# Two chained graph layers on one core: the short sums and a set of transposes change their place in each element's first slot, and the end of the last elements is rearranged

## The chip, the cores and the metric

The kernel runs on one core of a Trainium2 chip. The metric is device time in microseconds (us). The program is one launch that works through 32 batch elements. The core has a matrix engine (TensorE, PE in the profile, with its weight loads as PEld), a vector engine (VectorE, DVE), a scalar engine (ScalarE, ACT), GpSimd (POOL, not used in the loop) and SyncE (SP), which issues all transfers.

## The reference, cut to what matters

Everything is float32; a batch has 32 elements, each with 512 rows of 512 columns and a 512 x 512 matrix `adj`.

Layer 0 is attention with 8 heads of 64 columns. From x come q, k and v (products with three weights). The logits are q kᵀ/8 plus log(max(adj, 1e-8)); after the softmax the product with v, the product with Wo, and a layer norm of x plus the result give the rows n.

Layer 1 is graph attention on n with the same `adj`. Each row has one number q and one number k (dot products with two vectors). The logit of a pair is q + k, with (1 - adj) times -1e9 added, then a leaky ReLU with slope 0.01 and a softmax over the row. The weights e, times n, times fc, plus n, are the output:

```
logits = q + swapaxes(k)
masked = logits + (1 - adj) * -1e9
masked = where(masked >= 0, masked, 0.01 * masked)
out    = softmax(masked) @ (n @ fc^T + fc_b) + n
```

## The kernel before, in words

The order of each engine's work is written by hand: inside the kernel the program order of the calls is the order of each engine's queue, and only data dependences (semaphores) hold an engine back. SP's queue of transfers is in that order too.

Each element b has four slots (`slot(b, p)`, p = 0 to 3), one per pair of heads. A slot computes the scores of its pair, in four blocks of 128 keys (`score`, L809: TensorE into a two-bank tile of `ps_s`, then ScalarE's exponential into `at`), multiplies them by adj (`factors`, L823, VectorE; half 0 is blocks 0 and 1, half 1 is blocks 2 and 3) and adds them up over the blocks (`sums`, L833). The product of the factors with v (`values`, L843) comes a slot later: slot p runs `values` of pair p - 1, and slot 0 that of the last pair of element b - 1. Each slot also computes the q and k of the next slot (`seven_qk`, L591), with seven products of half matrices in place of eight (Strassen's scheme, as for v, Wo and fc too); the parts are put together by ScalarE and VectorE. The tile f of these products takes the two `ps_s` tiles of the second scores (blocks 2 and 3), once their exponentials have been read.

The division of the softmax is made once for two pairs. `divide` (L864) sums the 128 partitions of `as` with a weight of ones (TensorE, tile ps: "the short sums"), ScalarE copies them into R, and two small transfers bring them into a compact form c. `divided` (L884) checks their range and takes reciprocals on VectorE, and three transfers spread them to R over all partitions. `scale` (L904) multiplies oT by R. `divide(b, 0)` stands in slot 2 of element b, `divided(b, 0)` in its slot 3; `divide(b, 2)` and `divided(b, 2)` stand in slot 0 of element b + 1, and `scale(b, 2)` in slot 1.

The elements overlap. While slots of element b run layer 0, the same slots hold work of elements b - 1 and b - 2:

- slot 0: the transposes of the second half of adj for b (`turn_a((2, 3))`, VectorE, in place in cT), the transposes of the weights of layer 1 of element b - 2 (`eT`, VectorE, in place in eP) and the product of these weights with n (`z`, TensorE, tile pz, evicted by ScalarE into L), then `rest_of_layer1` (VectorE: `yb` = n * gamma + cc in two operations of 128x2048, and the reciprocals of the sums);
- slot 1: the product with Wo of element b - 1 (`seven_wo`), its statistics for the layer norm;
- slot 2 (`layer1_rows`): the norm's rows of element b - 1, the numbers k and q of its layer 1, the product with fc of element b - 2 (`seven_out`, with two stores of 512 KB), the transposes of x of element b + 1;
- slot 3: v of element b + 1 and the softmax of layer 1 of element b - 1 (`softmax`). That ends with 16 transfers of 64 KB, which rearrange the 32 x 32 blocks of the weights from L1 into eP (`spread_blocks`, L142; at L147). VectorE then transposes within each block.

In slot 0 TensorE's order is: scores 0 and 1, `values` of the last pair, the short sums of element b - 1, scores 2 and 3, the products for q and k, z. VectorE's is: scale, first_difference, factors half 0, turn_a, factors half 1, eT, sums, the additions for q and k, divided, residual, invert.

The last element's fourth slot is `last_slot` (L1186). There is no next element, so what is left of elements 30 and 31 is done: the softmax of layer 1 of element 30, the transposes of its weights on TensorE (pt_e), the division of element 31 without transfers (`divide_here`), z of element 30, Wo of element 31 (`seven_wo` with banks from `other_banks`, L800), its norm and layer 1, and the last two outputs with direct products (`out_units`, L455, tile pg).

`other_banks` gives three banks: b and c are the two halves of one tile of `ps_s`, a is the tile of `ps_o`. A tile is the unit for which one engine waits for another.

`combine_right` (L192) prepares the combinations of fc for the seven products; it also overwrites the upper right quarter of fc by (lower right - upper right). `last_slot` restores that quarter with one subtraction before the direct products.

Of the kernel before, what the change touches and what calls it, by code (L numbers as in the profile page):

```python
# [9 lines left out]
FP = mybir.dt.float32  # L10
# [9 lines left out]
P = 128  # L20
# [10 lines left out]
def kernel(  # L31
# [54 lines left out]
    nc = tc.nc  # L86
# [67 lines left out]
    K = {}  # L154
# [323 lines left out]
    def fast(ctx):  # L478
# [76 lines left out]
        def turn_a(kcs):  # L555
            for kc in kcs:
                nc.vector.transpose(cT[:, kc, :], cT[:, kc, :])
# [242 lines left out]
        def other_banks(b):  # L800

            def tiles():
                f = ps_s.tile([P, 2, N], FP, tag="s", name=f"pw_{b}_bc")
                o = ps_o.tile([P, N], FP, tag="po", name=f"pw_{b}_a")
                return [t.rearrange("p (n f) -> p n f", n=KH)
                        for t in (f[:, 1, :], o, f[:, 0, :])]
            return tiles

        def score(b, p, kc):  # L809
# [54 lines left out]
        def divide(b, p):  # L864


            s = S[b]
            ps = ps_m.tile([P, N], FP, tag="m", name=f"ps_{b}_{p}")
            for h in range(4):
                nc.tensor.matmul(  # L870
                    ps[h * BL : (h + 1) * BL, :], ones[:, :BL], s["as", p + h // 2][:, h % 2, :],
                    start=True, stop=True,
                )
            s["R", p] = act.tile([P, 2, N], FP, tag="R", name=f"R_{b}_{p}")
            r = s["R", p][:, 0, :]
            nc.scalar.copy(r, ps)
            m = 4 * N // P
            d0 = dram.tile([4, N], FP, tag="d0", name=f"d0_{b}_{p}")
            nc.sync.dma_start(out=d0, in_=r.rearrange("(h r) n -> h r n", r=BL)[:, 0, :])
            c = small.tile([P, 2, m], FP, tag="c", name=f"c_{b}_{p}")  # L880
            nc.sync.dma_start(out=c[:, 0, :], in_=d0.rearrange("h (a m) -> (h a) m", m=m))
            s["c", p] = c
# [150 lines left out]
        def slot(b, p):  # L1033

            last, nxt = b - 1, b + 1
            if p == 1 and last >= 0:
                load_n(last)
            if p == 1 and nxt < B:  # L1040
                load_x(nxt)
            if p == 3:
                differences(nxt)
            for kc in (0, 1):
                score(b, p, kc)
            if p == 1 and last >= 0:
                wos, wo_adds = seven_wo(last, long_banks(last))
                run(wos[:1])
            run(values(b, p - 1) if p > 0 else values(last, 3) if last >= 0 else first_v[1:2])
            if p == 0 and last >= 0:  # L1050
                scale(last, 0)
                first_difference(last)
                divide(last, 2)
            factors(b, p, 0)
            if p == 1:
                sums(b, p, 0)
                if last >= 0:
                    scale(last, 2)
                    first_sum(last)
            if p == 2 and last >= 0:  # L1060
                norm = normalise_units(S[last], small, last)
                run(norm[:1])
            if p == 0 and b > 0:
                turn_a((2, 3))
            if p == 3:
                load_a(nxt, (0, 1))
                if last >= 0:
                    mask(S[last])
                if b == 0:
                    run(combine_qk()[1:])  # L1070
            for kc in (2, 3):
                score(b, p, kc)
            soft = softmax(last) if p == 3 and last >= 0 else []
            run(soft[:1])
            factors(b, p, 1)
            if p == 3 and last >= 0:
                divided(b, 0)
            if p == 2:
                divide(b, 0)
            if b == 0 and p < 3:  # L1080
                next_qk = qk(0, p + 1)
            elif p < 3:
                next_qk = seven_qk(b, p + 1)
            else:
                next_qk = seven_qk(nxt, 0)
            if p == 0:
                if b >= 2:
                    run(eT(b - 2))
                sums(b, p, 0)
                if b == 0:  # L1090
                    run(combine(K["wv"], K["v_s"])[:1] + combine_qk()[:1])
                run(next_qk)
                units = z(b - 2) if b >= 2 else [lambda: spread(ps_o)] if b == 1 else first_v[2:]
                run(units[:2])
                if last >= 0:
                    divided(last, 2)
                run(units[2:])
                if b == 1:
                    combine_right(K["fc"], K["fc_s"])
                if b == 0:  # L1100
                    run(combine(K["wv"], K["v_s"])[1:])
                if b >= 2:
                    rest_of_layer1(b - 2)
            if p == 1:
                sums(b, 0, 1)
                if last < 0:
                    sums(b, p, 1)
                    run(next_qk)
                    bias()
                else:  # L1110
                    for i in range(3):
                        wos[i + 1]()
                        run(wo_adds[i])
                        if i == 1:
                            sums(b, p, 1)
                        next_qk[i]()
                    next_qk[3]()
                    wos[4]()
                    run(wo_adds[3])
                    run(stats_units(S[last], small, last))  # L1120
            if p == 2:
                if b == 0:
                    combine_right(K["wo"], K["wo_s"])
                    run(next_qk)
                    run(xT(nxt))
                    sums(b, p, 0)
                    offset()
                    divided(b, 0)
                else:
                    layer1_rows(b, next_qk, norm[1:])  # L1130
            if p == 3:
                load_a(nxt, (2, 3))
                vs = seven_v(nxt)
                vs[0]()
                run(soft[1:2])
                next_qk[0]()
                vs[1]()
                next_qk[1]()
                run(soft[2:])
                sums(b, 2, 1)  # L1140
                vs[2]()
                next_qk[2]()
                next_qk[3]()
                vs[3]()
                turn_a((0, 1))
                sums(b, p, 0)
                sums(b, p, 1)

        def layer1_rows(b, next_qk, norm):

            last, nxt = b - 1, b + 1
            muls, adds = [], [[], [], [], []]
            next_qk[0]()
            run(norm[:2])
            next_qk[1]()
            run(norm[2:])
            sums(b, 2, 0)
            if b >= 2:  # L1160
                z_sums(b - 2)
                muls, adds = seven_out(b - 2)
            ks, qs = dots_units(S[last], small, S[b]["R", 0][:, 1, :], last)
            run(ks)
            store_k(S[last], small, dram, last)
            run(next_qk[2:])
            run(muls[:1] + adds[0])
            turns = xT(nxt) if nxt < B else [lambda: sums(b, 2, 1)]
            run(turns[:1] + muls[1:2] + adds[1][:1] + turns[1:])
            load_k(S[last], work(last)[:, 1, :])  # L1170
            run(adds[1][1:])
            load_e(last, 0)
            run(muls[2:3] + adds[2] + muls[3:])
            load_e(last, 1)
            run(adds[3][:1] + qs)
            if nxt == B:
                load_n(b)
                divided(b, 0)
            run(adds[3][1:])

        def run_out(units):
            for mul, add in units:
                mul()
                add()

        def last_slot():  # L1186


            b, last = B - 1, B - 2
# [2 lines left out]
            run(values(b, 2))  # L1192
            factors(b, 3, 0)
            sums(b, 3, 0)
            mask(S[last])
            for kc in (2, 3):
                score(b, 3, kc)
            factors(b, 3, 1)
            load_e(b)
            vs = values(b, 3)  # L1200
            vs[0]()
            run(softmax(last))
            vs[1]()
            here2, here3 = divide_here(b, 2), divide_here(b, 3)
            here2[0]()
            nc.vector.tensor_add(S[b]["as", 3], S[b]["as", 3], S[b]["at", 3, 2])
# [24 lines left out]
            wos[4]()  # L1231
            run(wo_adds[3])
            invert(S[last])
            fc12, fc22 = K["fc"][:, :KH, H:], K["fc"][:, KH:, H:]
            nc.vector.tensor_sub(fc12, fc22, fc12)
            run(stats_units(S[b], small, b))
            zs[1]()
            norm = normalise_units(S[b], small, b)
# [45 lines left out]
        for b in range(B):  # L1284
            for p in range(NPAIR):
                if b == B - 1 and p == 3:
                    flag = last_slot()
                else:
                    slot(b, p)
        return flag  # L1290


# [142 lines left out]
```

## Time and profile before

| | us |
|---|---|
| three runs | 3533.10, 3531.07, 3532.73 |
| median | 3532.73 |
| profiled execution, its own time | 3532.92 |
| its span, first to last instruction | 3531.1 |
| TensorE busy | 3488.3 |
| VectorE busy | 2817.0 |
| ScalarE busy | 1377.2 |
| from one element to the next, in the middle | 108.62 |

The rows of the profile give an engine, a line of the kernel (L870) and an operation with the tile that it writes and those that it reads. In the timeline each row is a group of like instructions in order of time: start, length, then engine, line, operation, operands, shape, and how many. A bracket at its end is the time for which the engine stood idle before it, and what ended that. In the list of waits the first number is the total in us, then how often, then the longest. A float32 product of 128 x 128 by 512 columns shows as two matmul instructions. The last row of the table is the distance of the first z matmuls of neighbouring elements.

### The profile page before, as it was taken

Reading aid. Unit: us, or ns where it says so; the run is one execution under the profiler, and the core shown is the slowest. Engines: PE = TensorE matmul, PEld = TensorE weight load, DVE = VectorE, ACT = ScalarE, POOL = GpSimd, SP = SyncE. Lnnn points to the kernel's source line nnn. Section 1 sums busy time; section 2 is a strip of 40 time slices with the busy share of each in tenths; the row PEclk is TensorE's granted clock in tenths of the full one; section 3 lists DMA queues with packets and bytes.
Section 4 is the critical chain, followed back from the end, with each engine's and each line's share of the span. In section 5 each row is a group of like instructions: output and inputs, shape, how many; then the busy total and the mean of one; then the engine's idle time right before and its main releaser. Section 6 shows DMA issues by size and latency. Waiting matters only on the chain.

```text
span 3531.1 us, 40900 instructions
## 1 busy us (share of the span) xinstructions
PE 3488.3 (99%) x14554; PEld 2196.2 (62%) x14554; DVE 2817.0 (80%) x4925; ACT 1377.2 (39%) x2339; POOL 0.9 (0%) x9
## 2 busy tenths in 40 slices
PE   9999999999999999999999999999999999999998
PEld 3666666665666566666666666566656666666654
DVE  6878888778877788787888877887778878788875
ACT  3343343334433443434334333444344343434432
POOL 0000000000000000000000000000000000000000
PEclk9999999999999999999999999999999999999999
DMA  4334343343333343333434234333334242343420
GB/s 114 53 60 87 64 81 64 55 87 81 65 75 61 69 87 64 76 64 60 87 64 81 63 55 87 82 63 76 62 67 87 62 78 64 59 87 64 81 75 28
DMA packets 880010, 250.82 MB, mean 71 GB/s; under 512 B 806716, under 2 KB 806972, under 8 KB 879800
## 3 DMA queue, kind: packets, MB, share of 16 engines
q1 hardware_dynamic: 879800, 248.15, 36.1%
q8 instruction: 117, 1.92, 0.2%
q14 instruction: 93, 0.76, 0.1%
HBM read 181.93 MB, written 34.65 MB: 61 GB/s over the span
## 4 chain that ended last, share of the span: by engine, by line
PE 75%; DVE 12%; SPq 5%; issue 3%; DMA 2%; ACT 2%; DVEq 0%; ACTq 0%
PE f L604 14%; PE pz L310 13%; PE sc L815 10%; PE po L853 9%; PE pw_a L205 6%; PE pw_o_a L205 4%; SPq L147 4%; DVE at L828 4%; PE pw_c L205 3%; PE pw_o_c L205 3%; PE pv_a L205 3%; PE pw_o_b L205 2%; DVE eP L535 2%; DMA eP<-L 2%; PE pw_b L205 2%
## 5 line engine op out<-in xcount | busy, mean ns | idle before, releaser
L828 DVE SCALAR_TENSOR_TENSOR at<-cT,at 128x1024 f32<-128x1024 f32 x512 | 600.9, 1215 | 278.8 <-ACT at L820 275.2
L820 ACT ACTIVATE at<-sc 128x1024 f32<-128x1024 f32 x512 | 496.7, 1022 | 601.5 <-PE sc L815 599.8
L815 PE MATMUL sc<-qT,kT 64*128 64x512 f32 x2048 | 509.9, 616 | 2.2 <-DVE kT L639 2.2
L853 PE MATMUL po<-at,v 128*64 128x512 f32 x2048 | 468.6, 599 | 0.9 <-DVE at L828 0.9
L310 PE MATMUL pz<-eP,n 128*128 128x512 f32 x960 | 420.0, 595 | 11.8 <-DVE eP L535 11.8
L815 PEld LDWEIGHTS sc<-qT,kT 64*128 64x128 f32 x2048 | 176.5, 186 | 284.3 <-issue 284.3
L853 PEld LDWEIGHTS po<-at,v 128*64 128x64 f32 x2048 | 135.6, 137 | 319.0 <-issue 313.9
L310 PEld LDWEIGHTS pz<-eP,n 128*128 128x128 f32 x960 | 179.9, 190 | 239.1 <-issue 215.2
L841 DVE TENSOR_TENSOR as<-as,at 128x1024 f32<-128x1024 f32 x254 | 310.2, 1222 | 5.4
L604 PE MATMUL f<-xT,wq 128*128 128x256 f32 x992 | 261.0, 386 | 8.3 <-ACT at L820 8.3
L604 PE MATMUL f<-T,qk_s 128*128 128x256 f32 x992 | 246.2, 381 | 0.0
L452 ACT COPY L<-pz 128x512 f32<-128x512 f32 x128 | 74.9, 586 | 418.9 <-PE pz L310 418.9
L604 PEld LDWEIGHTS f<-xT,wq 128*128 128x128 f32 x992 | 183.4, 190 | 82.4 <-ACT at L820 60.0
L604 PEld LDWEIGHTS f<-T,qk_s 128*128 128x128 f32 x992 | 185.7, 190 | 30.2 <-ACT at L820 5.8
L861 ACT COPY oT<-po 128x512 f32<-128x512 f32 x128 | 75.2, 588 | 287.6 <-PE po L853 287.6
L838 DVE TENSOR_TENSOR as<-at,at 128x1024 f32<-128x1024 f32 x128 | 153.8, 1201 | 1.1
L744 DVE TENSOR_TENSOR n<-pw_a,n 128x512 f32<-128x512 f32 x96 | 66.3, 691 | 99.4 <-PE pw_a L205 99.4
L627 ACT ACTIVATE qT<-f,bq 128x256 f32<-128x256 f32 x124 | 58.3, 470 | 220.3 <-PE f L604 220.3
L633 ACT ACTIVATE kT<-f,bk 128x256 f32<-128x256 f32 x124 | 58.5, 472 | 196.4 <-PE f L604 196.4
L604 PE MATMUL f<-xT,qk_s 128*128 128x256 f32 x496 | 127.3, 379 | 0.0
L604 PE MATMUL f<-T,wk 128*128 128x256 f32 x496 | 127.3, 379 | 0.0
L604 PE MATMUL f<-xT,wk 128*128 128x256 f32 x496 | 127.3, 379 | 0.0
(239 smaller groups left out, 5350.5 us busy)
## 6 DMA issues: line engine op xcount, KB each, us to landing
cT<-in_adj_dram SPq DMA_DIRECT2D x512, 64.0 KB
R<-d SPq DMA_DIRECT2D x126, 256.0 KB
x<-in_x_dram SPq DMA_DIRECT2D x124, 256.0 KB
n<-in_x_dram SPq DMA_DIRECT2D x31, 1024.0 KB
L<-in_adj_dram SPq DMA_DIRECT2D x60, 512.0 KB
eP<-L SPq DMA_DIRECT2D x480, 64.0 KB
out_dram<-yb SPq DMA_DIRECT2D x60, 512.0 KB
w<-dk SPq DMA_DIRECT2D x32, 256.0 KB
```

What stands on the lines that cost most here:

```text
L147: nc.sync.dma_start(out=dst[j * BL : (j + 1) * BL, :, :].rearrange("r c (t q f) -> q r (c t) f", q=P // BL, f=BL)[i], in_=src[i * BL : (i ...
L205: nc.tensor.matmul(to[:, n, :], data(i, c)[:, ts(n, P)], weights[i][:, c, :], start=(first and n == 0 and c == 0), stop=(n == KH - 1 and c ...
L310: nc.tensor.matmul(ps, lhs(i), rhs(i), start=(i == 0), stop=(i == 3))
L452: nc.scalar.copy(s["zT"][:, d, :], pz)
L604: nc.tensor.matmul(to, left[i][:, c, ts(p, P)], s["B"][i][:, c, :], start=(first and c == 0), stop=(c == KH - 1), skip_group_check=True,)
L815: nc.tensor.matmul(sc[:, j, :], s["kT", p][rows, ts(kc, P)], s["qT", p][rows, :], start=True, stop=True,)
L820: nc.scalar.activation(at, sc, AF.Exp, scale=SCALE)
L828: nc.vector.scalar_tensor_tensor(at, cT[:, kc, :].unsqueeze(1).to_broadcast([P, 2, N]), ADJ_MIN, at, ALU.max, ALU.mult,)
L838: nc.vector.tensor_add(s["as", p], s["at", p, 0], s["at", p, 1])
L841: nc.vector.tensor_add(s["as", p], s["as", p], s["at", p, kc])
L853: nc.tensor.matmul(s["po", p][j * DK : (j + 1) * DK, :], s["v"][h // 4][:, kc, ts(h % 4, DK)], s["at", p, kc][:, j, :], start=(kc == 0), s ...
L861: nc.scalar.copy(s["oT"][p], s["po", p])
```

## The change

Three things are done.

In slot 0, for every element after the first, `divide` of the element before and `turn_a((2, 3))` move from ahead of the second scores to behind them, and `eT` moves from behind the second factors to ahead of turn_a. VectorE's order becomes: scale, first_difference, factors half 0, eT, turn_a, factors half 1, sums, the additions for q and k. TensorE's becomes: scores 0 and 1, values, scores 2 and 3, the short sums, q and k, z. `divided` moves from behind the second z unit to the end of the slot, behind `rest_of_layer1`.

At the last element, slot 2 leaves out the seven products for the output of element 29 (and the two sums on z that they need) and computes that output with `out_units`, four direct rows with one store of 256 KB each. Three rows run in slot 2, the fourth in `last_slot`. The upper right quarter of fc is restored at the start of that slot 2. The weights' input e of element 30 is loaded in one transfer instead of two. In `last_slot` the mask of element 30 goes behind the second factors, and both halves of the last product with v go ahead of its softmax.

`other_banks` takes three tiles: a and b are the first banks of two `ps_s` tiles, c is the tile of `ps_o`.

```diff
         def other_banks(b):
 
             def tiles():
-                f = ps_s.tile([P, 2, N], FP, tag="s", name=f"pw_{b}_bc")
-                o = ps_o.tile([P, N], FP, tag="po", name=f"pw_{b}_a")
-                return [t.rearrange("p (n f) -> p n f", n=KH)
-                        for t in (f[:, 1, :], o, f[:, 0, :])]
+                f = [ps_s.tile([P, 2, N], FP, tag="s", name=f"pw_{b}_{i}")[:, 0, :] for i in "ab"]
+                o = ps_o.tile([P, N], FP, tag="po", name=f"pw_{b}_c")
+                return [t.rearrange("p (n f) -> p n f", n=KH) for t in (f[1], f[0], o)]
             return tiles
...
             if p == 0 and last >= 0:
                 scale(last, 0)
                 first_difference(last)
-                divide(last, 2)
             factors(b, p, 0)
...
-            if p == 0 and b > 0:
-                turn_a((2, 3))
...
             soft = softmax(last) if p == 3 and last >= 0 else []
             run(soft[:1])
+            if p == 0 and last >= 0:
+                if b >= 2:
+                    run(eT(b - 2))
+                turn_a((2, 3))
+                divide(last, 2)
             factors(b, p, 1)
...
             if p == 0:
-                if b >= 2:
-                    run(eT(b - 2))
                 sums(b, p, 0)
...
-                run(units[:2])
-                if last >= 0:
-                    divided(last, 2)
-                run(units[2:])
+                run(units)
...
                 if b >= 2:
                     rest_of_layer1(b - 2)
+                if last >= 0:
+                    divided(last, 2)
...
-                    layer1_rows(b, next_qk, norm[1:])
+                    return layer1_rows(b, next_qk, norm[1:])
...
             last, nxt = b - 1, b + 1
+            if nxt == B:
+                fc12, fc22 = K["fc"][:, :KH, H:], K["fc"][:, KH:, H:]
+                nc.vector.tensor_sub(fc12, fc22, fc12)
...
-            if b >= 2:
+            if b >= 2 and nxt < B:
                 z_sums(b - 2)
                 muls, adds = seven_out(b - 2)
...
             run(next_qk[2:])
+            if nxt == B:
+                outs = out_units(S[b - 2], out[b - 2], ps_m, b - 2)
+                sums(b, 2, 1)
+                outs[0][0]()
+                load_k(S[last], work(last)[:, 1, :])
+                load_e(last)
+                load_n(b)
+                outs[0][1]()
+                run_out(outs[1:2])
+                run(qs)
+                divided(b, 0)
+                run_out(outs[2:3])
+                return outs[3]
...
-        def last_slot():
+        def last_slot(rest):
...
             sums(b, 3, 0)
-            mask(S[last])
             for kc in (2, 3):
                 score(b, 3, kc)
             factors(b, 3, 1)
             load_e(b)
+            mask(S[last])
             vs = values(b, 3)
             vs[0]()
+            vs[1]()
+            rest[0]()
             run(softmax(last))
-            vs[1]()
+            rest[1]()
...
-            fc12, fc22 = K["fc"][:, :KH, H:], K["fc"][:, KH:, H:]
-            nc.vector.tensor_sub(fc12, fc22, fc12)
             run(stats_units(S[b], small, b))
```

More of the change, by code (lines that the diff above doesn't have):

```diff
@@ L1166, in layer1_rows @@
             run(next_qk[2:])
+            if nxt == B:
[11 more added lines that the diff above has]
+                return outs[3]
             run(muls[:1] + adds[0])
-            turns = xT(nxt) if nxt < B else [lambda: sums(b, 2, 1)]
+            turns = xT(nxt)
             run(turns[:1] + muls[1:2] + adds[1][:1] + turns[1:])
@@ L1174, in layer1_rows @@
             load_e(last, 1)
[L1175 to L1179, printed above, removed]
+            run(adds[3][:1] + qs + adds[3][1:])
         def run_out(units):
@@ L1286, in fast @@
                 if b == B - 1 and p == 3:
-                    flag = last_slot()
+                    flag = last_slot(rest)
                 else:
-                    slot(b, p)
+                    rest = slot(b, p)
         return flag
```

## The prediction

> **What bounds the kernel now.** I read the page first. TensorE is busy in 99% of the span and has most of the chain that ended last; no other engine comes near.
>
> ```profile
> PE 3488.3 (99%) x14554; PEld 2196.2 (62%) x14554; DVE 2817.0 (80%) x4925; ACT 1377.2 (39%) x2339; POOL 0.9 (0%) x9
> ```
>
> So the span moves only with TensorE's own order of work, and 1% of idle time looks like all there is to win. The list of waits, read next, says otherwise. Its columns are total us, times, longest; there are 32 batch elements.
>
> ```profile
> PEld ps L870 <- DVE as L841: 19.8, 31, 0.6
> ...
> PE pz L310 <- DVE eP L535: 11.8, 30, 0.4
> PE f L604 <- ACT at L820: 8.3, 31, 0.3
> ```
>
> Three waits come once per element, and the first is one of the weight load, inside a stretch that counts as busy. All three lie in the first slot (p = 0). The timeline of TensorE there, element at 1062 us (start, length, then the group):
>
> ```profile
> 1067.64 1.84 PE L870 MATMUL ps<-as,ones 128*32 128x512 f32 x8
> 1069.41 1.99 PE L815 MATMUL sc<-qT,kT 64*128 64x512 f32 x8
> 1071.66 1.13 PE L604 MATMUL f<-xT,wq 128*128 128x256 f32 x4 [0.27 <-ACT at L820]
> ...
> 1074.41 1.03 PE L604 MATMUL f<-xT,wq 128*128 128x256 f32 x4
> 1075.28 1.03 PE L604 MATMUL f<-T,wk 128*128 128x256 f32 x4
> 1076.14 1.03 PE L604 MATMUL f<-xT,qk_s 128*128 128x256 f32 x4
> 1077.00 1.03 PE L604 MATMUL f<-xT,wk 128*128 128x256 f32 x4
> 1078.42 14.00 PE L310 MATMUL pz<-eP,n 128*128 128x512 f32 x32 [0.39 <-DVE eP L535]
> ```
>
> The third slot (p = 2) of the same element already has the order that the change gives the first: second scores, short sums, then the next q and k.
>
> ```profile
> 1014.99 1.99 PE L815 MATMUL sc<-qT,kT 64*128 64x512 f32 x8
> 1016.90 1.07 PE L870 MATMUL ps<-as,ones 128*32 128x512 f32 x8
> 1017.90 1.13 PE L604 MATMUL f<-xT,wq 128*128 128x256 f32 x4
> 1018.87 1.89 PE L604 MATMUL f<-T,qk_s 128*128 128x256 f32 x8
> 1020.59 1.03 PE L604 MATMUL f<-xT,wq 128*128 128x256 f32 x4
> ...
> 1024.05 1.89 PE L205 MATMUL pw_o_a<-fc,L 128*128 128x256 f32 x8
> ```
>
> Start to start, the same sums take 1.00 us there against 1.77, and no score waits. VectorE in the first slot:
>
> ```profile
> 1070.16 2.35 DVE L828 SCALAR_TENSOR_TENSOR at<-cT,at 128x1024 f32<-128x1024 f32 x2
> ...
> 1072.43 1.29 DVE L557 STREAM_TRANSPOSE cT<-cT 128x512 f32<-128x512 f32 x2
> ...
> 1073.65 2.31 DVE L828 SCALAR_TENSOR_TENSOR at<-cT,at 128x1024 f32<-128x1024 f32 x2
> ...
> 1075.89 2.48 DVE L535 STREAM_TRANSPOSE eP<-eP 128x512 f32<-128x512 f32 x4
> ...
> 1094.59 2.36 DVE L828 SCALAR_TENSOR_TENSOR at<-cT,at 128x1024 f32<-128x1024 f32 x2 [8.97 <-ACT at L820]
> ```
>
> It is late for the transposes of eP, yet stands idle 8.97 us before the next slot: its order is wrong, not its load. Last, the end of the program, where TensorE is not full:
>
> ```profile
> 3442.50 0.33 PE L303 MATMUL pt_e<-ident,qk_s 128*128 128x128 f32 x1 [2.62 <-ACT qk_s L431]
> ...
> 3458.49 1.99 PE L205 MATMUL pw_bc<-wo,oT 128*128 128x256 f32 x8 [1.44 <-DVE n L744]
> ```
>
> [...]0.64 us of waiting hides in a busy stretch of 1.84 us.[...] here banks b and c lie in one tile (pw_bc), and TensorE waited 1.44 and 1.38 us for VectorE to read it.[...] the clock reads 1.00 in all 110-us stretches between 220 and 3410 us and 0.93 in 3431 to 3480, where after the wait of 2.62 us four instructions of sums took 1.98 us, before it 1.03.[...]
>
> **The change, part by part.** Times are those of the element at 1062 us.
>
> *Short sums behind the second scores (31 elements).* They wait for the head sums of the last pair, which VectorE ends at 1068.36. Moved behind the scores they start at 1067.64 + 1.92 = 1069.56, later than that: 1.77 becomes 1.00, -0.77. In their new place they fill the time in which the first q/k group waited for ScalarE to empty the scores' banks: scores to that group is 2.25 us now, 1.91 + 1.00 there, so -0.34 beyond the sums themselves; the second group takes 1.78 now, 1.72 there, -0.06. Together -1.17 (6.77 us from 1067.64 to 1074.41; 5.60 in slot 2). ScalarE's copy of the sums goes behind two exponentials, as in slot 2, where nothing waits for it. The two small transfers behind it are issued about 1 us later and needed only when the reciprocals are taken.
>
> *eP's transposes ahead of the second factors (30 elements).* They start where the transposes of cT did, at 1072.43, and end 2.48 us later at 1074.9. z's first matmul would be free at 1067.64 + 2.91 + 6.15 = 1076.70 (both spans from slot 2), so it waits no more: 1.42 us from the last q/k group to z become 0.87, -0.55. The condition is that the 16 block transfers have landed: the last issue ends at 1069.49, and in windows of half a us over all 30 elements their traffic ends by 10.0 us after the slot's first score (1072.1) in most and by 11.0 in all; z feels it from 12.1. Behind the waiting transposes stand those of cT, the second factors, one sum and the three additions to q and k. The second transposes of cT and the second factors end 2.5 us later (1078.5), covered by z's 14 us: the next scores want the banks that the additions free at 1090.6, the product with v reads the factors at 1096. Without that cover each us late would cost one.
>
> Sum: -1.72, taken as -1.71, times 30 = -51.3 us.
>
> *Reciprocals behind the residual.* VectorE's work in the slot is the same, so `divided` ends at 1085.7 instead of 1081.06. It took 5.4 us from there until R had landed (traffic gone at 1086.5), so R is there at 1091.1; scaling in slot 1 now begins at 1098.12, then 1096.4. Margin 5.3 us, cost nothing. On SP only the loads of n and x are queued behind R's two issues; n waits for z until 1090.7, and R is issued by 1088.5.
>
> *Element 1* has no z to hide it: four operations of 2.65 us (`combine_right`) go ahead of `divided`, and R took 6.5 us there (123.98 to 130.47) and already held VectorE 0.35 us. New end 125.65, R at 132.1, scaling done at 133.4; the second weight product wants it at 131.1. Loss 2.3, less the 1.17 of the first part: +1.2 us.
>
> *Last elements.* Element 29's output is now four direct rows of 3.48 us (32 instructions of pg took 14.11) instead of seven products of 1.73 (12.96 with waits): three rows, 10.45, in slot 2 (-2.5) and the fourth in the hole of 2.62 us. That is 1.9 us more for TensorE, but what bounds here is the softmax of element 30 on VectorE. It loses z's two sums, has four operations on the output for sixteen, and one mask (1.22) no longer ahead of the factors; it gains the subtraction on fc (0.66) early, which stood before the statistics. But ScalarE now copies oT first (ready at 3435.4): I get logits 0.8 us earlier. The whole e and n are loaded some 7 us sooner on SP, with their readers at 3434 and later; four stores of 256 KB take the place of two of 512. Filling the hole spares the half clock. With three tiles, the second waiting for both tiles of sums to be read (over by 3452 now), the waits of 1.44 and 1.38 go; then VectorE's row of adds and residuals, some 12 us, sets the pace. The statistics start at about 3468.2 instead of 3472.67: -4.5 us, bounds -7 and +2 (the extra product uncovered), and all behind follows.
>
> Sum: -51.3 + 1.2 - 4.5 = -54.6 us, on the profiled execution 3531.1 of span and 3532.92 in all. The median of the runs, 3532.73, is within 0.2 of that: 3478.1.
>
> **Rivals.**
> A, eP lands late. VectorE then waits at the transposes and z starts no earlier. For: SP issues these 16 without a pause and they are in the chain that ended last. Against: 11.0 us at most, 12.1 to be felt. Price 30 x 0.55: 3494.6.
> B, the gain is given back at another wait, such as TensorE for VectorE in the next slot. For: VectorE has no gap in this slot. Against: 8.97 us of idle time before slot 1, of which 1.7 go. Time about 3529.
> C, slower: R lands late. Its place is the scaling ahead of the second weight product in slot 1. It decides from 5.3 us late, and the kernel is slower than before from 5.3 + 54.6/30 = 7.1. That needs R's transfers stuck behind the 1 MB of n and the blocks of x; 8 us late gives 30 x (2.7 - 1.71) - 3.3 = +26: 3559. Against: R is issued first, and with x issued right behind it at element 1 it was 1.1 us slower, not 7.
>
> **How the numbers follow.** Forecast 0.76 (its own range 3471 to 3486: 0.15 us per element and 3 at the end), A 0.13, B 0.06, C 0.05. The range 3468 to 3496 takes in the forecast and A. A measurement of this kernel can tell about 0.2%, 7 us. Faster: 0.76 + 0.13 + a third of B = 0.91; same: the rest of B, 0.04; slower: C, 0.05.
>
> **What would show it.** Right: sums of 1.07 us behind the scores in slot 0, no wait of f for ScalarE nor of pz for eP, a period of 106.9 instead of 108.6 us, VectorE idle some 7.3 us before slot 1, no wait of pw on pw_b or pw_c. Wrong: a wait for eP's transfers at L535 on VectorE (A), of oT for R (C), or a clock below 1.00 in the middle: at 0.983 the whole gain is gone.

## The result and the profile after

The changed kernel takes 3475.75 us (median of four runs, 3474.64 to 3476.18), against 3532.45 for the kernel before (four runs, 3531.07 to 3533.10): a ratio of 0.984, 95% interval 0.9822 to 0.9857. The forecast was 3478.1 in a range of 3468 to 3496. The profiled execution has a span of 3473.5 us, 57.6 less than before.

The page of the changed kernel, its rows of busy time and of the chain that ended last (before, TensorE had 75% of that chain and VectorE 12%):

```profile
PE 3451.6 (99%) x14530; PEld 2193.0 (63%) x14530; DVE 2813.1 (81%) x4911; ACT 1375.9 (40%) x2338; POOL 1.0 (0%) x9
...
PE 97%; DVE 2%; DMA 1%; ACT 0%; issue 0%; SPq 0%; DVEq 0%; ACTq 0%
```

TensorE's busy share reads 99% as before, though 36.7 us of busy time are gone: 24 of them are the short sums (67.1 us for 504 instructions, 91.0 before). The waits of TensorE, longest first (total us, times, longest):

```profile
PE pt_x L551 <- DMA n<-in_x_dram: 3.6, 1, 3.6
PE pw_c L205 <- DVE oT L921: 2.7, 1, 2.7
PE pt_e L303 <- ACT qk_s L431: 2.5, 4, 1.4
PE sc L814 <- DVE kT L639: 2.2, 1, 2.2
PE pt_e L303 <- ACT cT L431: 1.9, 4, 0.8
```

No wait comes once per element any more; f for the exponential and pz for eP are gone from the list, and so is the weight load of the sums for `as`. TensorE in slot 0, in the timeline of an element in the middle (start, length, group):

```profile
1048.22 1.99 PE L814 MATMUL sc<-qT,kT 64*128 64x512 f32 x8
1050.14 3.65 PE L852 MATMUL po<-at,v 128*64 128x512 f32 x16
1053.72 1.99 PE L814 MATMUL sc<-qT,kT 64*128 64x512 f32 x8
1055.64 1.06 PE L869 MATMUL ps<-as,ones 128*32 128x512 f32 x8
1056.64 1.13 PE L604 MATMUL f<-xT,wq 128*128 128x256 f32 x4
1057.61 1.89 PE L604 MATMUL f<-T,qk_s 128*128 128x256 f32 x8
...
1061.92 1.03 PE L604 MATMUL f<-xT,wk 128*128 128x256 f32 x4
1062.79 13.90 PE L310 MATMUL pz<-eP,n 128*128 128x512 f32 x32
1076.61 1.99 PE L814 MATMUL sc<-qT,kT 64*128 64x512 f32 x8
```

From the slot's first score to z are 14.57 us; before, 16.28. VectorE in the same slot:

```profile
1056.25 2.35 DVE L827 SCALAR_TENSOR_TENSOR at<-cT,at 128x1024 f32<-128x1024 f32 x2
1058.52 2.48 DVE L535 STREAM_TRANSPOSE eP<-eP 128x512 f32<-128x512 f32 x4
1060.93 1.26 DVE L557 STREAM_TRANSPOSE cT<-cT 128x512 f32<-128x512 f32 x2
1062.12 2.31 DVE L827 SCALAR_TENSOR_TENSOR at<-cT,at 128x1024 f32<-128x1024 f32 x2
...
1071.49 0.25 DVE L893 RECIPROCAL c<-c 128x16 f32<-128x16 f32 x1
1078.84 2.36 DVE L827 SCALAR_TENSOR_TENSOR at<-cT,at 128x1024 f32<-128x1024 f32 x2 [7.10 <-ACT at L819]
...
1082.38 1.28 DVE L907 TENSOR_TENSOR oT<-oT,R 128x512 f32<-128x512 f32 x2
```

The transposes of eP follow the first factors without a wait here and end 1.8 us before z begins. (In a few of the 30 elements VectorE waits for eP's transfers after all, 1.2 us in sum and 0.6 at most; z starts 14.56 us after the first score there too.) The idle time before slot 1 is down from 8.97 to 7.10 us: that is the room that the gain came from. The scaling by R does not wait.

At the end of the program, the transposes of elements 30 and 31 (TensorE, same view):

```profile
3387.28 0.33 PE L303 MATMUL pt_e<-ident,qk_s 128*128 128x128 f32 x1 [1.36 <-ACT qk_s L431]
...
3389.40 2.92 PE L303 MATMUL pt_e<-ident,qk_s 128*128 128x128 f32 x13 [0.38 <-ACT qk_s L431]
...
3437.34 3.04 PE L303 MATMUL pt_e<-ident,cT 128*128 128x128 f32 x13 [0.38 <-ACT cT L431]
```

The hole ahead of the first is 1.36 us instead of 2.62. The last group took 1.66 us before and takes 3.04 now.

Where the 57.6 us of span came from:

| part | before | after | gain |
|---|---|---|---|
| one element to the next (eight periods, z to z) | 108.616 | 106.789 | 1.83 x 30 = 54.8 |
| element 1, its first score to that of element 2 | 89.04 | 89.06 | 0.0 |
| last z of eP to the end (the gain without the 0.1 in z itself) | 171.73 | 167.98 | 3.6 |
| start to the first score of element 1 | 104.17 | 104.86 | -0.7 |

The last row has nothing of the change in it: with the same start, the other kernels of this study read 103.7 to 104.8 there.

### The profile page after: what moved, and what is told of

The parts are those of the page before. It is cut to its first block, busy times and chain, and to the rows that moved or that the text cites. A ratio compares the mean times of both kernels' runs of the same rounds, so it can differ in the third digit from the quotient of the medians.

```text
span 3473.5 us, 40744 instructions
## 1 busy us (share of the span) xinstructions
PE 3451.6 (99%) x14530; PEld 2193.0 (63%) x14530; DVE 2813.1 (81%) x4911; ACT 1375.9 (40%) x2338; POOL 1.0 (0%) x9
## 4 chain that ended last, share of the span: by engine, by line
PE 97%; DVE 2%; DMA 1%; ACT 0%; issue 0%; SPq 0%; DVEq 0%; ACTq 0%
PE f L604 22%; PE sc L814 14%; PE po L852 13%; PE pz L310 12%; PE pw_a L205 6%; PE pv_a L205 5%; PE pw_o_a L205 4%; PE pw_c L205 3%; PE pv_b L205 3%; PE pv_c L205 3%; PE pw_o_b L205 3%; PE pw_o_c L205 3%; PE ps L869 2%; PE pw_b L205 2%; PE pg L310 1%; PE pk L310 0%
```

## The experiments

The theory: the two moves in slot 0 release the same z from two sides, TensorE's and VectorE's, and only together give 1.83 us; the later place of `divided` is covered by other work; the end is worth 3 to 4 us. Rivals: the parts add up one by one; the transfers of eP or of R set the time.

### The sums alone, the transposes alone

```diff
                 first_difference(last)
-                divide(last, 2)
...
             run(soft[:1])
+            if p == 0 and last >= 0:
+                divide(last, 2)
             factors(b, p, 1)
```

> Of the change only this: the short sums go behind the second scores in slot 0; VectorE's order and everything else stay as before. Theory (the two moves in slot 0 interlock): the wait of the sums' weight load and the 0.27 us of f for ScalarE go, so q and k are done 1.17 us earlier, but VectorE ends the transposes of eP at the same time as before, so z starts no earlier: the wait of pz for eP grows from 0.39 to about 1.6 us, and the time stays within 4 us of before (about 3531). Rival (the parts add up): 1.17 us for each of 31 elements, about 3496.

Measured: 3532.88 us, ratio 0.9999 (0.9991 to 1.0008). TensorE in slot 0 of this kernel:

```profile
1067.10 1.07 PE L870 MATMUL ps<-as,ones 128*32 128x512 f32 x8
1068.09 1.13 PE L604 MATMUL f<-xT,wq 128*128 128x256 f32 x4
...
1075.96 14.00 PE L310 MATMUL pz<-eP,n 128*128 128x512 f32 x32 [1.56 <-DVE eP L535]
```

The sums are as short as in the whole change and f waits for nothing, but z now waits 1.56 us for eP. From the first score (1059.68) it is 16.28 us to z, to the hundredth what it was before. So 1.17 us for each of 30 elements were won and lost again 8 us later: a second wait stood behind the first.

```diff
             if p == 0 and b > 0:
+                if b >= 2:
+                    run(eT(b - 2))
                 turn_a((2, 3))
...
             if p == 0:
-                if b >= 2:
-                    run(eT(b - 2))
                 sums(b, p, 0)
```

> Of the change only this: eP's transposes go ahead of those of cT and of the second factors on VectorE; the short sums stay ahead of the second scores. Theory: only z's wait goes, 0.55 to 0.66 us for each of 30 elements: 3513 to 3516, with the sums still at 1.84 us. Rival (the blocks of eP land late): VectorE waits at the transposes and z starts as before, about 3532.

Measured: 3513.29 us, ratio 0.9946 (0.993 to 0.9961).

```profile
1060.12 1.84 PE L870 MATMUL ps<-as,ones 128*32 128x512 f32 x8
...
1064.14 1.13 PE L604 MATMUL f<-xT,wq 128*128 128x256 f32 x4 [0.27 <-ACT at L820]
...
1070.34 13.90 PE L310 MATMUL pz<-eP,n 128*128 128x512 f32 x32
```

z starts 15.72 us after the first score (1054.62), 0.56 sooner, and takes 0.1 less itself: 0.66 x 30 = 20 us. One part is worth 0, the other 20 us, both 54 (next run, which also has the reciprocals' move; that is worth nothing at these elements, as shown further below). The additive rival, 3496 for the sums, is excluded.

### All of slot 0, and the end alone

The first of these kernels has the whole diff for slot 0 and nothing of the end; the second is its complement.

> All of the change in slot 0 (sums, transposes, reciprocals at the end of the slot), and the end of the last elements as before. Theory: 30 elements at 1.8 us, element 1 at nothing: 3478 to 3480, so that the end is worth 3 to 4 us in the whole change. Rival: the end carries more than 8 us of the change, because it works with the new order: above 3484.

> The end of the last elements as changed (direct rows for element 29, three bank tiles), and slot 0 as before. Theory: 3 to 4 us faster, 3528 to 3530. Rival: the direct rows (1.9 us more of TensorE) and the new half clock at the end eat it, within 1 us of before.

Measured: 3479.38 us, ratio 0.985 (0.9835 to 0.9865), and 3528.72 us, ratio 0.9987 (0.998 to 0.9993). Against the 3533.04 of the kernel before in these runs that is 53.7 and 4.3 us, in sum 58.0, and the whole change is worth 56.7 or 57.3, by either measurement of the kernel before: these two parts, which lie at different places, add up within the spread of the runs.

### When eP's blocks have landed

```diff
                 first_difference(last)
+                if b >= 2:
+                    run(eT(b - 2))
             factors(b, p, 0)
...
             if p == 0 and last >= 0:
-                if b >= 2:
-                    run(eT(b - 2))
                 turn_a((2, 3))
```

> The whole change, with eP's transposes moved up once more, ahead of the first factors of slot 0. This measures when the blocks have landed: VectorE should stand idle at L535 for eP's transfers in each of 30 elements, some 1.7 to 2.5 us, ending about 10 to 10.5 us after the slot's first score. Theory: covered all the same (z needs the transposes done 14.56 us after that score), time within 3 us of the change, 3473 to 3479. Rival (VectorE's order in slot 0 has no such room): each us of idle time costs up to one, 3500 and more.

Measured: 3477.85 us, ratio 0.9843 (0.9828 to 0.9859). VectorE's waits at these transposes come to 49.5 us in 30 elements, at most 2.8; its timeline in one of them:

```profile
1061.38 2.49 DVE L535 STREAM_TRANSPOSE eP<-eP 128x512 f32<-128x512 f32 x4 [1.76 <-DMA eP<-L]
```

The slot's first score was at 1051.52, so the blocks were there after 9.86 us, in the worst element about 10.9. In the change the transposes are called for after 10.3. Standing idle 1.65 us on average cost nothing: from one element to the next it is 106.79 us in both kernels. (The median is 2.1 us above the change's. In the profile it is element 1 that takes longer, by 3.4 us; nothing of the move lies there.) So rival A of the prediction is out, and VectorE's order in this slot has the room that was claimed.

### R late

```diff
                 if b >= 2:
                     rest_of_layer1(b - 2)
+                    for _ in range(9):
+                        nc.vector.tensor_add(S[last]["R", 2][:, 1, :], K["gamma"], K["cc"])
                 if last >= 0:
                     divided(last, 2)
```

The additions write a half of R that the transfers behind the reciprocals overwrite. The second kernel has 12 of them.

> The whole change, with nine needless additions of 128x512 (0.69 us each, 6.2 us) on VectorE ahead of the reciprocals in slot 0, so that R lands 6.2 us later for 30 elements; they end before VectorE's next work. The prediction put the margin at 5.3 us. Theory: VectorE then waits 0.5 to 1.2 us for R at the scaling, but the second weight product wants it only 2 us after that, so TensorE loses nothing: within 4 us of the change, up to 3480. Rival (each us over the margin is a us lost): 0.9 us for each of 30, about 3503.

> As with nine, but twelve additions, 8.3 us: R 8.3 us later, and VectorE about 1.2 us late for the first factors of slot 1. Theory: now TensorE waits for the scaled oT in slot 1, about 0.9 us at the second weight product and up to 1 us behind it: 3500 to 3535. Rival: still covered, within 4 us of the change.

Measured: 3505.73 us, ratio 0.992 (0.9904 to 0.9935), and 3589.76 us, ratio 1.0155 (1.014 to 1.0171). Both theories fell: with nine the rival's figure held (3503), and twelve cost 55 us more than the upper end of its range. VectorE and TensorE with nine:

```profile
1087.94 0.25 DVE L893 RECIPROCAL c<-c 128x16 f32<-128x16 f32 x1
...
1094.99 1.29 DVE L907 TENSOR_TENSOR oT<-oT,R 128x512 f32<-128x512 f32 x2 [2.49 <-DMA R<-d]
```

```profile
1096.76 1.97 PE L205 MATMUL pw_c<-wo_s,oT 128*128 128x256 f32 x8 [0.70 <-ACT pw_b L697]
```

The reciprocals end 29.93 us after the slot's first score, 6.4 later than in the change. But R then takes 6.8 us to land, not 5.4. Its two transfers are issued from 1089.64 to 1090.94 here, directly ahead of those of n and x (at 1091.04 and 1091.68); whether that is why, no run isolates. So VectorE waits 2.5 us where the margin of the prediction gave 1.1; the weight product was wanted at 1095.90 and starts 0.86 late. (The profile names ScalarE here, whose copy into pw_b ended just before. But in the change this product starts while that copy has yet to begin, so it doesn't need it, and at 26 of 32 such waits with nine additions the profile names VectorE's L921, the differences behind the scaling.) 30 us in all, 1.0 per element. With twelve the reciprocals are 8.6 us late:

```profile
1120.20 2.52 PE L205 MATMUL pw_c<-wo_s,oT 128*128 128x256 f32 x8 [2.68 <-DVE oT L921]
1122.51 1.91 PE L604 MATMUL f<-xT,wq 128*128 128x256 f32 x4
```

To the wait of 2.68 comes here a loss of clock: four matmuls take 1.91 us instead of 1.03. Over the whole of this run the mean clock is 0.992, in the change 0.999. My range had counted 1.9 us per element; it is 3.8, of which the waits are 2.9. The kernel becomes slower than before between 6.4 and 8.6 us of lateness, which takes in the 7.1 of the prediction (rival C); its price for 8 us late, 3559, left out this loss of clock and R's longer landing (6.6 us here: the reciprocals end at 1111.85, the scaling starts at 1118.43).

### The reciprocals' place, and element 1

At element 1 the four operations on fc stand ahead of the reciprocals, and TensorE waited there 2.71 us. This kernel mends that alone:

```diff
                 if b == 1:
+                    divided(last, 2)
                     combine_right(K["fc"], K["fc_s"])
...
-                if last >= 0:
+                if b >= 2:
                     divided(last, 2)
```

> The whole change, but at element 1 alone the reciprocals stand ahead of the four operations on fc again. Theory: R lands there before the second weight product wants it, TensorE's wait of 2.71 us goes; but in the changed kernel this wait had been followed by no half clock at element 1's third slot, which in the kernel before cost 1.6 us, and that may come back: 0.5 to 3 us faster than the change, 3472 to 3475. Rival (the time at element 1 is set elsewhere): no difference, 3475 to 3476.

Another puts `divided` back to its old place at all elements:

> The whole change, but with the reciprocals in their old place (behind z's second unit, ahead of the residual) for all elements. Theory: moving them cost nothing but at element 1, so the time is that of the run that mends element 1 alone, within 2 us. Rival: behind the residual they cost something at every element (or they gained something there): more than 5 us away from that run.

Measured: 3473.01 us, ratio 0.9829 (0.9815 to 0.9842), and 3475.49 us (3472.47 to 3475.86), ratio 0.9835 (0.9821 to 0.9848). The medians lie 2.5 us apart, the spans of the profiled executions 0.6 (3471.2 and 3471.8), the intervals overlap. The medians miss the 2 us of my theory by half a us and stay within the 5 of the rival; the traces decide: from one element to the next both take 106.79 us, as the change does, so the place of the reciprocals costs nothing at every element. The mended element 1 in TensorE's timeline:

```profile
131.08 1.97 PE L205 MATMUL pw_c<-wo_s,oT 128*128 128x256 f32 x8
...
164.66 3.55 PE L814 MATMUL sc<-qT,kT 64*128 64x512 f32 x8 [2.18 <-DVE kT L639]
```

The wait of 2.71 us is gone, and half of it comes back: behind the wait of 2.18 us at the third slot, which all kernels have, the scores take 3.55 us here, 1.99 in the change and 3.10 before (the section on the clock has the clock of these two). From first score to first score element 1 takes 87.84 us, 1.2 less.

### One tile for two banks

`other_banks` as before, all else as changed.

> The whole change, but with the banks b and c of the last Wo product in one tile again. Theory: TensorE's two waits for VectorE to read that tile (1.44 and 1.38 us) come back, but VectorE's row of adds and residuals behind them has some slack, so 1.5 to 2.8 us slower than the change: 3477 to 3479. Rival: VectorE sets the pace there in any case: no difference to the change (3475 to 3476).

Measured: 3479.05 us, ratio 0.9847 (0.9834 to 0.986), 3.3 us above the change. Both waits are back:

```profile
3401.22 1.99 PE L205 MATMUL pw_bc<-wo,oT 128*128 128x256 f32 x8 [1.44 <-DVE n L744]
...
3406.32 1.99 PE L205 MATMUL pw_bc<-wo,oT 128*128 128x256 f32 x8 [1.38 <-DVE n L744]
```

From the last z of eP to the end this kernel takes 171.14 us, the change 168.0. So the 2.8 us of waits cost their whole length, a little more than the range of my theory, and are most of what the end gains: the statistics start 2.3 us later, and then VectorE waits another 1.1 for TensorE's z, which is late too. (The spans of the two profiled executions, 3475.3 and 3473.5, differ by less, because element 1 happened to start 1.2 us sooner here.) The intervals of the ratios overlap, the times themselves don't: 3477.1 is the lowest here, 3476.18 the highest of the change.

### The clock at the end

Four needless matmuls fill the gaps in which TensorE waits for the weights of element 31:

```diff
+                    nc.tensor.matmul(warm, ident, K["wq"][:, 0, :], start=True, stop=True)
                     for c in range(4):
                         nc.tensor.transpose(pt[:, ts(c, P)], s["e"][:, c, ts(0, P)], ident)
+                        if c < 3:
+                            nc.tensor.matmul(warm[:, :200], ident, K["wq"][:, 0, :200], start=True, stop=True)
```

> The whole change, with four needless matmuls put into the four gaps in which TensorE waits for the last element's weights to be exponentiated (0.75 and three times 0.38 us). Theory: the half clock after these gaps (13 transposes in 3.04 instead of 1.66 us, the first z row 3.90 instead of 3.69) comes from the idle time; filled, it stays at full clock: 1 to 2 us faster, 3473.5 to 3475. Rival: the transposes wait for ScalarE's copies, or the clock falls all the same: no difference or slower, 3475 to 3477.

> Element 1 mended and the gaps at the end filled, both on top of the change. Theory: the two gains add up, 2 to 5 us faster than the change, 3471 to 3474. Rival: [...]together they bring no more than one of them.

Measured: 3475.02 us, ratio 0.9835 (0.9821 to 0.9848), on the border of the theory and its rival, and with element 1 mended too 3471.97 us, ratio 0.9826 (0.9813 to 0.9839). The transposes of the first:

```profile
3438.67 0.33 PE L973 MATMUL pt_warm<-ident,cT 128*128 128x128 f32 x1
3438.84 1.50 PE L303 MATMUL pt_e<-ident,cT 128*128 128x128 f32 x12
3440.17 3.69 PE L310 MATMUL pz<-eT,n 128*128 128x512 f32 x8
```

From the first transpose to z are 3.62 us instead of 4.94. In the times the gain of 1.3 us is no more than their spread (in this profile the second weight product of element 1 took 3.64 us, 1.97 in the change's). Both mends together are the fastest kernel of the study, 3.8 us below the change; the intervals of the ratios still overlap.

In the change these 13 transposes take 3.04 us. The view of stretches gives busy time of TensorE, its weight load, VectorE, ScalarE and GpSimd, then the clock, and two columns on transfers. The stretch of the transposes in the change, then in the kernel with eP's transposes first, whose end is the same:

```profile
3437.34:3440.76 3.42, 3.42 (x14) 3.16 (x15) 1.23 (x2) 2.11 (x4) 0.00 (x0) 0.50 0.41 153
```

```profile
3439.86:3443.27 3.41, 2.92 (x17) 2.14 (x18) 1.22 (x3) 2.82 (x7) 0.00 (x0) 1.00 0.40 154
```

The gaps ahead are nearly the same (1.9 and 2.0 us in the lists of waits), and the clock read 0.50 in one trace and 1.00 in the other. In the kernel before, with a longer first gap (1.25 us and three times 0.38), it read 1.00 too, and the same transposes took 1.66 us. With the gaps filled it reads 1.00 from 3435.3 to 3441.3; that the filling kept it up can't be told from these kernels. The same holds at element 1's third slot. Behind the same wait of 2.19 us, in the kernel before and in the change:

```profile
166.56:169.97 3.41, 3.41 (x10) 0.92 (x8) 3.34 (x8) 2.05 (x2) 0.00 (x0) 0.50 0.15 44
```

```profile
167.37:170.78 3.41, 2.61 (x12) 1.12 (x14) 3.41 (x7) 1.44 (x2) 0.00 (x0) 1.00 0.02 5
```

What decides whether the clock falls, no run isolates.

## Why the prediction was right

**Sums behind the scores, -1.17.** The sums now take 1.06 where 1.00 was counted from start to start, f waits no more, and the second group follows in 0.97: as worked out. What the working left unsaid is that this part alone is worth nothing, because z would have waited for eP in its stead. The two amounts were priced one after the other and summed; the sum held only because both moves are in the change.

**Transposes ahead of the second factors, -0.55.** As worked out: z follows the last q/k group after 0.87 us. Mis-sized was z itself: its first matmul had taken 697 ns instead of 592, a part of the wait that counts as busy, so the whole of z went from 13.93 to 13.82. 1.71 was predicted for both, 1.83 measured: 3.5 us over 30 elements.

**Landing of eP.** Predicted by 10.0 us in most and 11.0 in all, 12.1 to be felt; measured 9.86 in one and 10.9 in the worst.

**Reciprocals behind the residual, 0.** They end 23.5 us after the slot's first score (1071.74 against 1048.22), the 23.56 of the prediction, and nothing waits for R. The margin of 5.3 us held by luck, from two errors. With nine additions R took 6.8 us to land instead of 5.4, so VectorE's scaling has a margin of only 3.9 us. But the second weight product is wanted 1.6 us after the scaling could first have served it (in the trace with nine additions, 1095.90 against an estimated 1094.27), so TensorE loses time only from about 5.5 us on, by this estimate.

**Element 1, +1.2.** (2.3 less 1.17 is 1.1.) The wait was 2.71 us against 2.3. R landed as predicted, 28.0 us after the element's first score; but the second weight product waits not only for the scaling, as counted, but for the first of the differences behind it (L921; the product starts 0.5 us after the scaling's end). Still the element lost nothing: before, a half clock had followed the wait at its third slot (clock 0.50, scores of 3.10 and products of 4.19 us), and in the changed kernel it did not (1.00, 1.99 and 3.65). That term was not in the sum, and it is luck: nothing in the change aims at it, and with element 1 mended the scores take 3.55 us again.

**Last elements, -4.5.** Measured -3.6. The statistics start 108.36 us after the last z of eP began, 113.30 before: 4.9 sooner, against 4.5 predicted. The step that failed is "filling the hole spares the half clock". The hole shrank to 1.36 us and three gaps of 0.38, and behind them the clock still read 0.50, for 3.42 us (from 3389.55) where it had been 6.83 (from 3443.35 in the kernel before); and at the very end, where the clock had been full, it fell too, which took back 1.6 us (1.4 in the transposes, 0.2 in z). The latter is chance rather than the change: in the kernel with eP's transposes first, whose end is the same, the clock stayed at 1.00 there and the stretch from the last z took 166.4 us instead of 168.0.

Sum: -51.3 + 1.2 - 4.5 = -54.6 predicted; -54.8 + 0.0 - 3.6 = -58.4 measured by parts, with 0.7 of the start on the other side. Rivals A and B did not come; C needs the reciprocals to be about 7 us later than the change has them. That measurement and forecast lie as close as 2.4 us owes something to chance: the terms that were off (z itself, element 1, the end, the start) are of that size and go both ways.

## What to carry to other kernels

When two engines meet at one instruction, ask of each move what the other engine will hold back instead: here one move alone was worth 0, the other 20 us, and both 54. A busy share of 99% can hide such room; compare a stretch with another stretch of the same kernel that does the same work in a better order, and price the difference from start to start. Before putting a step later, look not only at how long its transfers take now but at which transfers will then be issued beside them (with n and x issued right behind, R took 6.8 us here instead of 5.4).

## What the runs showed that I had not expected

The clock of TensorE read 0.50 for 3.4 us behind idle time shorter than that, and not each time: behind a wait of 2.2 us at one and the same place of element 1 eight scores took 1.99 us in the change, 2.49 with both mends, 3.10 in the kernel before and 3.55 with element 1 mended. Gaps of 0.75 and three times 0.38 us, with short transposes between them, came ahead of 0.50 at the end of the change; 1.25 and three times 0.38 did not cost the kernel before anything there. So in these traces a wait cost its own length and up to 1.7 us more (at element 1 of the kernel with the end filled the second weight product took 3.64 us behind its wait, 1.97 in the change), and where that came shifted from kernel to kernel; of the last 3 us of a sum one should not be sure.
